# Cross attention: first scores, weighing of the batch ahead and second scores as one block of small products; transposes and low parts moved

## The chip, the cores and the metric

The kernel runs on one core of a Trainium2 chip. The time is device microseconds of one launch; the kernel before took 896.02 us (median of 3 runs, 895.63 to 896.3). The profile is of one further execution of it. Five engines work side by side: TensorE (PE in the profile, its weight loads PEld), VectorE (DVE), ScalarE (ACT), GpSimd (POOL) and SyncE (SP), which only issues transfers here. Each runs its own instructions in order and waits on semaphores for the others.

## The reference

One layer of three blocks with residuals: cross attention of 64 latents a batch to 512 context rows and to themselves, self attention over the 64 latents, and a feed forward part whose inputs and weights are rounded to 4-bit blocks. There are 16 batches, the width is 512. The change touches the first block only:

```python
xn = _ln(x, g_x, b_x)            # the context: 16 x 512 x 512
ln = _ln(latents, g_l, b_l)      # the latents: 16 x 64 x 512
q = ln @ w_q
kv_in = jnp.concatenate([xn, ln], axis=1)
k, v = jnp.split(kv_in @ w_kv, 2, axis=-1)
q, k, v = (split(q) * scale, split(k), split(v))     # 8 heads of 64
sim = jnp.einsum('bhid,bhjd->bhij', q, k)
sim = jnp.where(m, sim, -jnp.finfo(sim.dtype).max)
attn = jax.nn.softmax(sim, axis=-1)
out = jnp.einsum('bhij,bhjd->bhid', attn, v)
return _ln(out @ w_out, g_o, b_o)
```

## The kernel before

The program has three stages. `_latents` makes keys, queries and values of the latents and the context weights; `cross_attention` runs over the 16 batches; `SelfAttention` and `FeedForward` follow, tile by tile of 128 latent rows. The order of the instructions on each engine is the order in which the functions below call them; nothing reorders them between engines except the semaphore waits.

A matrix product to near fp32 is three products of high and low parts (`terms`, L121: high x high, high x low, low x high), with 4 slices of 128 in the inner dimension: twelve matmuls of 128 x 512 make one "full product" below.

In `cross_attention` batch b has:

- `keys(b, m)`, m = 0 to 3: a full product of two heads' keys, 128 x 512 (tile `pk`), then VectorE multiplies it with the row of inverse deviations (L911, tile `k`). The first and last 64 columns of `k` are keys of the latents, fetched by `around` (four small transfers for two m). There are six homes for `k`, four of which a batch takes; so the fetch for m = 2, 3 of the next batch must wait for this batch's first scores, and that for m = 0, 1 of the batch after for its second scores.
- `values(b, t)`, t = 0 to 3: a full product of 128 context rows' values (`pv`), which ScalarE scales and copies to `v` (L924).
- `scores(b, a)`, a = 0, 1: 8 small matmuls (16 passes in the trace) of 64 x 64 weights by 288 columns into two score tiles of two banks each (`sim`). a = 0 needs keys 0 and 1, a = 1 keys 2 and 3.
- `softmax(b, a)`: VectorE subtracts, masks and takes the minimum, twice (L956, out of `sim` into `pr`), ScalarE takes the exponential and its sum, twice (L960).
- `turn` and `turn_both`: eight transposes of `pr` in all for each a (`prt`, L171), ScalarE copies them to `prT` (L972). `turn_latents` transposes the latents' part (`prlt`, L989), ScalarE copies it to `prl`.
- `finish(b)`: `weigh`, 40 small matmuls (80 passes) with 128 x 64 tiles into the bank `av` (L1005), then `collect` on VectorE (a reciprocal L1017 and two products L1023).
- every second batch, for a pair `done` of finished batches: `out_turn` (four transposes `ot`, ScalarE's high part `oh` L1038, VectorE's low part `ol` L1041), `out_product` (a full product `po`), `out_norm`, `out_add`.

The eight banks of TensorE's output memory are split in three pools: `ps_mm`, three banks for full products and transposes (`mm`, `tr`); `ps_sim`, two tiles of two banks (`two`); `ps_av`, one bank.

Between these, in the same order, stand the preparation of the next batch's context (`cx.high` on ScalarE, `cx.low` on VectorE for even and on GpSimd for odd slices, L362 and L368; `cx.stats`, L321; `cx.fetch`, `cx.flat`, `cx.every` transfers) and `tick()`, which advances the rounding of the feed forward weights by one step (`Quantise.piece`: VectorE, GpSimd and ScalarE ops L194 to L210 and L287 to L290, two transfers).

The weighing of batch b - 1 happens inside batch b. The order of the small products in a batch before: after keys 0 and 1 the transposes of `pr` 1 and of the latents of batch b - 1 (and `ot`); after keys 2 the weighing of b - 1 and the first scores of b; after keys 3 and values 0 and 1 the transposes of `pr` 0 and the second scores of b.

Of the kernel before, what the change touches and what calls it, by code (L numbers as in the profile page):

```python
# [9 lines left out]
F32 = mybir.dt.float32  # L10
# [9 lines left out]
P = 128  # L20
D = 512
KC = D // P
B = 16
S = 64
N = 512
NJ = N // P
NT = B * S // P
# [18 lines left out]
def f32(t):  # L46

    return t.bitcast(F32)
# [777 lines left out]
def cross_attention(tc, cm, sc, i, cw, cx, w1, w2, att, quant):  # L826

    nc = tc.nc
# [19 lines left out]
    def columns_of(r):  # L848

        first = S * (1 - r)  # L850
        return slice(first, first + N + S), slice(S - first, S - first + N)

    state = {}
# [48 lines left out]
    def keys(b, m):  # L902

        k = ends.pop((b, m))
        hi, lo = cx.done[b]
        cols = slice(m * P, (m + 1) * P)
        ps = cm.mm(f"pk_{b}_{m}")
        cm.product(
            ps, lambda c: (w_k[0][:, c, cols], w_k[1][:, c, cols], hi[:, c, :], lo[:, c, :]), range(KC)
        )  # L910
        nc.vector.tensor_tensor(k[:, S : S + N], ps, cx.row[b], ALU.mult)  # L911
        state[b]["k"].append(k)
# [14 lines left out]
    def scores(b, a):  # L927

        st = state[b]
        st["sim", a] = pss = [cm.two(f"sim_{b}_{a}_{r}") for r in range(2)]  # L930
        for h in range(2):
            for r in range(2):
                rows = slice(r * S, (r + 1) * S)
                at = columns_of(r)[0].start + h * half
                for c in range(2):
                    m = 2 * a + c
                    nc.tensor.matmul(  # L937
                        pss[r][c * S : (c + 1) * S, h, :half],
                        lhsT=queries[b % 2][rows, m, :],
                        rhs=st["k"][m][rows, at : at + half],  # L940
                        start=True,
                        stop=True,
                    )

    def softmax(b, a):
        st = state[b]
        st["pr", a] = w1.tile([P, 2, N + S], F32, tag="pr", bufs=2, name=f"pr_{b}_{a}")

        def two(t):
            return t.rearrange("p (h n) -> p h n", h=2)  # L950

        for r, ps in enumerate(st.pop(("sim", a))):
            mask = masks[b % 2][:, columns_of(r)[0]]
            pr = st["pr", a][:, r, :]
            least = cm.small.tile([P, 1], F32, tag="least", name=f"least_{b}_{a}_{r}")
            nc.vector.tensor_tensor_reduce(  # L956
                two(pr), ps[:, :, :half], two(mask), -1.0, BIG, ALU.add, ALU.min, least
            )
            t = 2 * a + r
            nc.scalar.activation(  # L960
                pr, pr, AF.Exp, bias=least, scale=-1.0, accum_out=st["tot"][:, t : t + 1]
            )

    def turn(b, a, r):
        st = state[b]
        pt = cm.tr(f"prt_{b}_{a}_{r}")
        cm.transpose_chunks(pt, st["pr", a][:, r, columns_of(r)[1]], NJ)
        turned(b, a, r, pt)

    def turned(b, a, r, pt):  # L970
        prT = w1.tile([P, NJ, P], F32, tag="prT", bufs=4, name=f"prT_{b}_{a}_{r}")
        nc.scalar.copy(prT, pt.rearrange("p (j q) -> p j q", q=P))  # L972
        state[b]["prT", a, r] = prT

    def turn_both(b):

        pt = cm.two(f"prt_{b}")
        for r in range(2):
            cm.transpose_chunks(pt[:, r, :], state[b]["pr", 1][:, r, columns_of(r)[1]], NJ)
        for r in range(2):  # L980
            turned(b, 1, r, pt[:, r, :])

    def turn_latents(b):
        st = state[b]
        prl = w2.tile([P, 2, P], F32, tag="two_h", bufs=2, name=f"prl_{b}")
        pt = cm.tr(f"prlt_{b}")[:, : 2 * P].rearrange("p (n q) -> p n q", q=P)
        for a in range(2):
            pr = st.pop(("pr", a)).rearrange("p r t -> p (r t)")
            nc.tensor.transpose(pt[:, a, :], pr[:, N : N + P], cm.ident)  # L989
        nc.scalar.copy(prl, pt)  # L990
        st["prl"] = prl
# [38 lines left out]
    def out_turn(p):  # L1030
        o = state.pop(("o", p))
        pt = cm.tr(f"ot_{p}")
        cm.transpose_chunks(pt, o.rearrange("p a c r d -> p (a c r d)"), KC)
        oh = w1.tile([P, KC, P], F32R, tag="oh", name=f"oh_{p}")
        ol = w2.tile([P, KC, P], F32R, tag="ol", name=f"ol_{p}")
        for k in range(KC):
            src, bias = pt[:, k * P : (k + 1) * P], cw.bv[:, k : k + 1]
            nc.scalar.activation(oh[:, k, :], src, AF.Identity, bias=bias)  # L1038
        for k in range(KC):
            src, bias = pt[:, k * P : (k + 1) * P], cw.bv[:, k : k + 1]  # L1040
            nc.vector.scalar_tensor_tensor(  # L1041
                ol[:, k, :], src, bias, f32(oh[:, k, :]), ALU.add, ALU.subtract
            )
        state["oT", p] = oh, ol

    def out_product(p):
        oh, ol = state.pop(("oT", p))
        po = cm.mm(f"po_{p}")
        cm.product(
            po, lambda k: (oh[:, k, :], ol[:, k, :], w_o[0][:, k, :], w_o[1][:, k, :]), range(KC)  # L1050
        )
        state["po", p] = po, cm.moments(po, f"o_{p}")
# [13 lines left out]
    def out_moments(p):  # L1066
        cm.shift(cm.x[p], f"a_{p}", cm.x_mv[:, p, :])
# [12 lines left out]
    def finish(b):  # L1080
        for a in range(2):
            for r in range(2):
                weigh(b, a, r)
        collect(b)
# [11 lines left out]
    for b in range(B):  # L1096

        def tick():
            if b:
                quant.tick()  # L1100

        done = (b - 3) // 2 if b >= 3 and b % 2 else None
        last = b == B - 1
        keys(b, 0)
        if last:
            att.load("Wq")
            att.load("Wk")
        cx.high(b + 1, 0)
        if b >= 4 and b % 2 == 0:
            out_moments((b - 4) // 2)  # L1110
        if b > 1:
            tick()
        keys(b, 1)
        cx.low(b + 1, 0)
        cx.high(b + 1, 1)
        if b > 1:
            tick()
        if b:
            turn_both(b - 1)
            turn_latents(b - 1)  # L1120
        if done is not None:
            out_turn(done)
        keys(b, 2)
        cx.fetch(b + 2, 0)
        if b == 0:
            for k in range(KC):
                load_o(k)
        cx.flat(b + 1)
        cx.low(b + 1, 1)
        cx.high(b + 1, 2)  # L1130
        tick()
        if last:
            att.split("Wq", 0, 1)
        if b:
            finish(b - 1)
        tick()
        if last:
            att.split("Wq", 2)
        scores(b, 0)
        softmax(b, 0)  # L1140
        around(b + 1, 2, 3)
        keys(b, 3)
        cx.fetch(b + 2, 1)
        cx.low(b + 1, 2)
        cx.high(b + 1, 3)
        tick()
        values(b, 0)
        cx.every(b + 1)
        cx.low(b + 1, 3)
        cx.stats(b + 2, 0)  # L1150
        tick()
        if last:
            att.split("Wq", 3)
            att.load("Wv")
        values(b, 1)
        begin(b + 1)
        latents_values(b + 1)
        cx.fetch(b + 2, 2)
        cx.stats(b + 2, 1)
        tick()  # L1160
        if last:
            att.norm(0)
            att.split("Wk", 0, 1)
        turn(b, 0, 0)
        turn(b, 0, 1)
        scores(b, 1)
        softmax(b, 1)
        around(b + 2, 0, 1)
        if done is not None:
            out_product(done)  # L1170
        tick()
        values(b, 2)
        cx.fetch(b + 2, 3)
        cx.stats(b + 2, 2)
        tick()
        if done is not None:
            out_norm(done)
            out_add(done)
        if b == 0:
            weight_o(0)  # L1180
            weight_o(1)
        if b == 2:
            att.sa.load()
        if b == 5:
            att.sa.work()
        if last:
            att.split("Wk", 2, 3)
            att.load("Wo")
            att.turn(0)
        values(b, 3)  # L1190
        cx.stats(b + 2, 3)
        cx.spread(b + 2)
        mask(b + 1)
        if b == 0:
            weight_o(2)
            weight_o(3)
        quant.tick()
        cx.load(b + 3)
    turn_both(B - 1)
    turn_latents(B - 1)  # L1200
    att.product(0, "Wq")
    att.split("Wv", 0, 1)
# [4 lines left out]
    att.product(0, "Wk")  # L1207
    att.rope(0, "Wk")
    out_turn(NT - 1)
    att.product(0, "Wv")  # L1210
    out_moments(NT - 2)
    att.end(0)
# [678 lines left out]
```

## Time and profile before

| | |
|---|---|
| time, median of 3 runs (range) | 896.02 us (895.63 to 896.3) |
| the profiled execution: time, span from first to last instruction | 895.7 us, 893.9 us |
| two batches of cross attention in its trace (428.67 to 489.80 us) | 61.13 us |
| busy in these: TensorE, weight loads, VectorE, ScalarE, GpSimd | 61.13, 49.17, 50.52, 29.09, 26.20 us |
| granted TensorE clock | 0.999 |
| DMA busy share over these two batches | 0.52 |

A row of the profile's timeline gives start and length in us, engine, line, operation, the tile written and those read, array tile (rows\*columns), output shape and count; a last bracket tells how long the engine had stood idle before and what released it. Cross attention runs from about 84 to 574 us.

### The profile page before, as it was taken

How to read it: one execution, taken by the hardware profiler on the slowest of the kernel's cores; microseconds unless marked ns; L12 is line 12 of the kernel's file. 1: busy time of each engine (PE TensorE's matmuls, PEld its weight loads, DVE VectorE, ACT ScalarE, POOL GpSimd, SP SyncE). 2: the span in 40 equal slices, each digit the busy share in tenths (PEclk: the TensorE clock that was granted, in tenths of full speed). 3: DMA queues.
4: the chain of work that ended last, by engine and by line, in shares of the span. 5: the costliest groups of instructions: out<-in, count | busy, mean ns of one | idle time of the engine just before them, and what ended most of it. 6: DMA issues, size and time to landing. Idle time of an engine off the chain costs nothing.

```text
span 893.9 us, 17187 instructions
## 1 busy us (share of the span) xinstructions
PE 886.8 (99%) x6583; PEld 735.9 (82%) x6583; DVE 693.0 (78%) x1414; ACT 399.8 (45%) x785; POOL 305.7 (34%) x357
## 2 busy tenths in 40 slices
PE   8999999999999999999999999999999999999998
PEld 8998778877887878788778877878888888888887
DVE  7554467798799787786987985588998897888876
ACT  5553544543454445445444544555555323322221
POOL 3244233335253353162453532545444120100000
PEclk9999999999999999999999999999999999999999
DMA  8465554645565456445554442331006530000000
GB/s 294 155 236 165 169 155 138 186 143 154 158 179 144 153 150 176 117 133 156 144 156 152 137 126 97 116 148 43 1 1 251 198 142 13 12 12 12 12 13 24
DMA packets 80378, 111.11 MB, mean 124 GB/s; under 512 B 33176, under 2 KB 39080, under 8 KB 79016
## 3 DMA queue, kind: packets, MB, share of 16 engines
q1 hardware_dynamic: 80136, 109.48, 38.4%
q8 instruction: 52, 0.85, 0.4%
q0 software_dynamic: 160, 0.52, 0.2%
q14 instruction: 30, 0.25, 0.1%
HBM read 84.26 MB, written 25.72 MB: 123 GB/s over the span
## 4 chain that ended last, share of the span: by engine, by line
PE 96%; DVE 2%; POOL 1%; issue 0%; DMA 0%; ACT 0%; POOLq 0%; DVEq 0%; ACTq 0%
PE pk L121 20%; PE pv L121 20%; PE gu L121 14%; PE dn L121 7%; PE av L1005 5%; PE sim L937 4%; PE prt L171 3%; PE po L121 3%; PE Wv L121 2%; PE wo L121 2%; PE lv L121 2%; PE Wq L121 2%; PE Wk L121 2%; PE lq L121 2%; PE lk L121 2%; PE ht L171 1%
## 5 line engine op out<-in xcount | busy, mean ns | idle before, releaser
L121 PE MATMUL pv<-xvh,x 128*128 128x512 f32 x512 | 133.1, 392 | 0.0
L121 PE MATMUL pk<-x,xkh 128*128 128x512 f32 x512 | 130.4, 397 | 0.0
L121 PEld LDWEIGHTS pk<-x,xkh 128*128 128x128 f32 x512 | 93.7, 188 | 25.4 <-issue 3.9
L121 PEld LDWEIGHTS pv<-xvh,x 128*128 128x128 f32 x512 | 95.3, 188 | 23.3 <-issue 1.8
L911 DVE TENSOR_TENSOR k<-pk,row 128x512 f32<-128x512 f32 x64 | 43.9, 685 | 51.9 <-PE pk L121 51.9
L924 ACT ACTIVATE v<-pv,rs 128x512 f32<-128x512 f32 x64 | 43.9, 686 | 78.1 <-PE pv L121 78.0
L960 ACT ACTIVATE pr<-pr,least 128x576 f32<-128x576 f32 x64 | 49.2, 771 | 58.3 <-DVE least L956 56.7
L368 POOL TENSOR_TENSOR x<-raw,x 128x512 fp32r<-128x512 f32 x32 | 43.7, 1365 | 77.4 <-ACT x L362 71.1
L121 PE MATMUL pk<-x,xkl 128*128 128x512 f32 x256 | 68.7, 390 | 0.0
L121 PE MATMUL pv<-xvl,x 128*128 128x512 f32 x256 | 68.5, 389 | 0.0
L121 PE MATMUL gu<-uT,fx 128*128 128x512 f32 (+1 forms) x288 | 66.7, 377 | 0.0
L121 PE MATMUL gu<-gT,fx 128*128 128x512 f32 (+1 forms) x288 | 65.8, 376 | 0.0
L121 PEld LDWEIGHTS gu<-gT,fx 128*128 128x128 f32 x288 | 52.2, 188 | 7.6 <-ACT fx L129 0.2
L121 PEld LDWEIGHTS gu<-uT,fx 128*128 128x128 f32 x288 | 51.9, 188 | 7.2
L121 PEld LDWEIGHTS pk<-x,xkl 128*128 128x128 f32 x256 | 48.0, 188 | 10.4
L121 PEld LDWEIGHTS pv<-xvl,x 128*128 128x128 f32 x256 | 48.1, 188 | 10.2
L956 DVE CUSTOM_DVE_ANT_0 pr<-sim,mask 128x576 f32<-128x576 f32 x64 | 45.9, 754 | 6.5 <-PE sim L937 5.3
L205 ACT ACTIVATE qe_h<-qe_h,mmagic 128x512 f32<-128x512 f32 (+1 forms) x24 | 16.5, 688 | 66.4 <-DVE qe_h L202 64.3
L321 DVE BATCH_NORM_STATS2 cst<-nat 128x6 f32<-128x512 f32 x64 | 42.9, 670 | 3.5 <-DMA nat<-in_ctx_dram 3.5
L121 PE MATMUL dn<-dT,hh 128*128 128x512 f32 x170 | 42.9, 392 | 0.0
L972 ACT COPY prT<-prt 128x512 f32<-128x512 f32 x64 | 34.1, 585 | 18.4 <-PE prt L171 18.4
L1005 PEld LDWEIGHTS av<-v,prT 128*64 128x64 f32 x1024 | 36.7, 138 | 5.6 <-issue 5.6
(339 smaller groups left out, 1959.0 us busy)
## 6 DMA issues: line engine op xcount, KB each, us to landing
nat<-in_ctx_dram SPq DMA_DIRECT2D x16, 1024.0 KB
raw<-in_ctxT_dram SPq DMA_DIRECT2D x64, 256.0 KB
d_d<-qhl_d SPq DMA_DIRECT2D x11, 512.0 KB
row<-rs_d SPq DMA_DIRECT2D x16, 256.0 KB
g_d<-qhl_g SPq DMA_DIRECT2D x8, 512.0 KB
u_d<-qhl_u SPq DMA_DIRECT2D x8, 512.0 KB
gT<-g_d SPq DMA_DIRECT2D x4, 1024.0 KB
uT<-u_d SPq DMA_DIRECT2D x4, 1024.0 KB
```

The lines of the kernel that those rows point to most:

```text
L121: self.nc.tensor.matmul(ps, lhsT=p[i], rhs=p[j], start=start and n == 0, stop=stop and n == last)
L171: self.nc.tensor.transpose(pt[:, c * P : (c + 1) * P], src[:, c * P : (c + 1) * P], self.ident)
L205: nc.scalar.activation(e, e, AF.Relu, bias=self.mmagic, scale=MAGIC)
L321: nc.vector.bn_stats(st, self.nat[b][:, j, :])
L368: by.tensor_tensor(lo, self.raw[:, c, :], f32(hi), ALU.subtract)
L911: nc.vector.tensor_tensor(k[:, S : S + N], ps, cx.row[b], ALU.mult)
L924: nc.scalar.mul(v, ps, cx.rs[b][:, t : t + 1])
L937: nc.tensor.matmul(pss[r][c * S : (c + 1) * S, h, :half], lhsT=queries[b % 2][rows, m, :], rhs=st["k"][m][rows, at : at + half], start=Tru ...
L956: nc.vector.tensor_tensor_reduce(two(pr), ps[:, :, :half], two(mask), -1.0, BIG, ALU.add, ALU.min, least)
L960: nc.scalar.activation(pr, pr, AF.Exp, bias=least, scale=-1.0, accum_out=st["tot"][:, t : t + 1])
L972: nc.scalar.copy(prT, pt.rearrange("p (j q) -> p j q", q=P))
L1005: nc.tensor.matmul(st["av"][rows, 2 * a + r, :], lhsT=w[:, rows], rhs=v[:, at : at + S], start=(n == 0), stop=(n == len(pairs) - 1),)
```

## The change

The two forms of turning `pr` become one, `turn(b, a)`, whose eight transposes go into one score tile. `turn_latents` uses the bank of the weighing. `out_turn` is split: its VectorE part becomes `out_low`. In the loop over the batches:

- `turn(b - 1, 1)`, `turn_latents(b - 1)` and `out_turn` move from behind keys 1 to behind keys 0; `out_low` stands behind keys 1.
- first scores, weighing of b - 1 and second scores stand together behind keys 3 and ahead of values 0, with both `around` fetches behind them. (Batch 0, with nothing to weigh, has its first scores behind keys 2, its second behind values 0.)
- `turn(b, 0)` stays behind values 1, without the second scores; one `tick()` moves from behind `finish` to behind `turn(b, 0)`; in the last batch `att.split("Wq", 2)` moves behind keys 3.

```diff
@@ -961,29 +961,21 @@
                 pr, pr, AF.Exp, bias=least, scale=-1.0, accum_out=st["tot"][:, t : t + 1]
             )
 
-    def turn(b, a, r):
-        st = state[b]
-        pt = cm.tr(f"prt_{b}_{a}_{r}")
-        cm.transpose_chunks(pt, st["pr", a][:, r, columns_of(r)[1]], NJ)
-        turned(b, a, r, pt)
-
-    def turned(b, a, r, pt):
-        prT = w1.tile([P, NJ, P], F32, tag="prT", bufs=4, name=f"prT_{b}_{a}_{r}")
-        nc.scalar.copy(prT, pt.rearrange("p (j q) -> p j q", q=P))
-        state[b]["prT", a, r] = prT
-
-    def turn_both(b):
-
-        pt = cm.two(f"prt_{b}")
+    def turn(b, a):
+
+        pt = cm.two(f"prt_{b}_{a}")
         for r in range(2):
-            cm.transpose_chunks(pt[:, r, :], state[b]["pr", 1][:, r, columns_of(r)[1]], NJ)
+            cm.transpose_chunks(pt[:, r, :], state[b]["pr", a][:, r, columns_of(r)[1]], NJ)
         for r in range(2):
-            turned(b, 1, r, pt[:, r, :])
+            prT = w1.tile([P, NJ, P], F32, tag="prT", bufs=4, name=f"prT_{b}_{a}_{r}")
+            nc.scalar.copy(prT, pt[:, r, :].rearrange("p (j q) -> p j q", q=P))
+            state[b]["prT", a, r] = prT
 
     def turn_latents(b):
         st = state[b]
         prl = w2.tile([P, 2, P], F32, tag="two_h", bufs=2, name=f"prl_{b}")
-        pt = cm.tr(f"prlt_{b}")[:, : 2 * P].rearrange("p (n q) -> p n q", q=P)
+        pt = cm.ps_av.tile([P, D], F32, tag="av", name=f"prlt_{b}")[:, : 2 * P]
+        pt = pt.rearrange("p (n q) -> p n q", q=P)
         for a in range(2):
             pr = st.pop(("pr", a)).rearrange("p r t -> p (r t)")
             nc.tensor.transpose(pt[:, a, :], pr[:, N : N + P], cm.ident)
@@ -1036,15 +1028,18 @@
         for k in range(KC):
             src, bias = pt[:, k * P : (k + 1) * P], cw.bv[:, k : k + 1]
             nc.scalar.activation(oh[:, k, :], src, AF.Identity, bias=bias)
+        state["oT", p] = oh, ol, pt
+
+    def out_low(p):
+        oh, ol, pt = state["oT", p]
         for k in range(KC):
             src, bias = pt[:, k * P : (k + 1) * P], cw.bv[:, k : k + 1]
             nc.vector.scalar_tensor_tensor(
                 ol[:, k, :], src, bias, f32(oh[:, k, :]), ALU.add, ALU.subtract
             )
-        state["oT", p] = oh, ol
 
     def out_product(p):
-        oh, ol = state.pop(("oT", p))
+        oh, ol, _ = state.pop(("oT", p))
         po = cm.mm(f"po_{p}")
         cm.product(
             po, lambda k: (oh[:, k, :], ol[:, k, :], w_o[0][:, k, :], w_o[1][:, k, :]), range(KC)
@@ -1110,16 +1105,18 @@
             out_moments((b - 4) // 2)
         if b > 1:
             tick()
+        if b:
+            turn(b - 1, 1)
+            turn_latents(b - 1)
+        if done is not None:
+            out_turn(done)
         keys(b, 1)
+        if done is not None:
+            out_low(done)
         cx.low(b + 1, 0)
         cx.high(b + 1, 1)
         if b > 1:
             tick()
-        if b:
-            turn_both(b - 1)
-            turn_latents(b - 1)
-        if done is not None:
-            out_turn(done)
         keys(b, 2)
         cx.fetch(b + 2, 0)
         if b == 0:
@@ -1131,18 +1128,23 @@
         tick()
         if last:
             att.split("Wq", 0, 1)
-        if b:
-            finish(b - 1)
-        tick()
-        if last:
-            att.split("Wq", 2)
-        scores(b, 0)
-        softmax(b, 0)
-        around(b + 1, 2, 3)
+        if b == 0:
+            scores(b, 0)
+            softmax(b, 0)
         keys(b, 3)
         cx.fetch(b + 2, 1)
         cx.low(b + 1, 2)
         cx.high(b + 1, 3)
+        if last:
+            att.split("Wq", 2)
+        if b:
+            scores(b, 0)
+            softmax(b, 0)
+            finish(b - 1)
+            scores(b, 1)
+            softmax(b, 1)
+            around(b + 1, 2, 3)
+            around(b + 2, 0, 1)
         tick()
         values(b, 0)
         cx.every(b + 1)
@@ -1152,6 +1154,11 @@
         if last:
             att.split("Wq", 3)
             att.load("Wv")
+        if b == 0:
+            scores(b, 1)
+            softmax(b, 1)
+            around(b + 1, 2, 3)
+            around(b + 2, 0, 1)
         values(b, 1)
         begin(b + 1)
         latents_values(b + 1)
@@ -1161,11 +1168,8 @@
         if last:
             att.norm(0)
             att.split("Wk", 0, 1)
-        turn(b, 0, 0)
-        turn(b, 0, 1)
-        scores(b, 1)
-        softmax(b, 1)
-        around(b + 2, 0, 1)
+        turn(b, 0)
+        tick()
         if done is not None:
             out_product(done)
         tick()
@@ -1196,7 +1200,7 @@
             weight_o(3)
         quant.tick()
         cx.load(b + 3)
-    turn_both(B - 1)
+    turn(B - 1, 1)
     turn_latents(B - 1)
     att.product(0, "Wq")
     att.split("Wv", 0, 1)
@@ -1207,6 +1211,7 @@
     att.product(0, "Wk")
     att.rope(0, "Wk")
     out_turn(NT - 1)
+    out_low(NT - 1)
     att.product(0, "Wv")
     out_moments(NT - 2)
     att.end(0)
```

## The prediction

> **What bounds the kernel now.** I read the page from the top: busy shares, clock row, chain of waits; then TensorE's timeline over one batch, then VectorE's over the next, because the change reorders one engine and leans on the other.
>
> ```profile
> PE 886.8 (99%) x6583; PEld 735.9 (82%) x6583; DVE 693.0 (78%) x1414; ACT 399.8 (45%) x785; POOL 305.7 (34%) x357
> PEclk9999999999999999999999999999999999999999
> PE 96%; DVE 2%; POOL 1%; issue 0%; DMA 0%; ACT 0%; POOLq 0%; DVEq 0%; ACTq 0%
> ```
>
> TensorE is busy 99% of the span at the full granted clock and is 96% of the chain. So time is won only by making its stream shorter, and lost only by making it wait. The stream, batch b = 10 (start, length, what):
>
> ```profile
> 388.81 1.03 PE L171 MATMUL prt<-ident,pr 128*128 128x128 f32 x8
> 389.69 0.38 PE L989 MATMUL prlt<-ident,pr 128*128 128x128 f32 x2
> 389.82 2.09 PE L121 MATMUL pk<-x,xkh 128*128 128x512 f32 x8
> ...
> 392.75 0.57 PE L1005 MATMUL av<-v,prT 128*64 128x64 f32 x12
> ...
> 395.23 1.20 PE L937 MATMUL sim<-k,mask 64*64 64x288 f32 x16
> 396.36 2.11 PE L121 MATMUL pk<-x,xkh 128*128 128x512 f32 x8
> ...
> 399.23 1.07 PE L121 MATMUL pv<-xvh,x 128*128 128x512 f32 x4
> ...
> 404.68 1.03 PE L171 MATMUL prt<-ident,pr 128*128 128x128 f32 x8
> 405.64 1.20 PE L937 MATMUL sim<-k,mask 64*64 64x288 f32 x16
> 406.77 1.20 PE L121 MATMUL pv<-xvh,x 128*128 128x512 f32 x4
> ...
> 412.35 1.98 PE L121 MATMUL pk<-x,xkh 128*128 128x512 f32 x8
> ```
>
> Read starts, not lengths (matmuls overlap). The 24 key products from 412.35 end where the next transposes start, 417.79: 5.44 us, 0.2267 each, 2.72 for a product of twelve. Whatever a stretch takes beyond that is the price of small products and of going in and out of them. The full-array products need no help; what the array's tile (128\*128, 128\*64, 64\*64 in the rows) changes to is what costs.
>
> **The change, part by part.** First TensorE, before:
>
> - 388.81 to 392.75: 3.94, less 2.72 = 1.22 for ten transposes and the way into the 128\*64 tile. Of that the way in is about 0.08: the first 36 key products of batch 0 (83.88 to 92.13) take 8.25 against 36 x 0.2267 = 8.16, so 0.09 into 64\*64; and transposes cost 0.11 each (388.81 to 389.69) plus 0.06 at their edge (four of them and a product, 576.76 to 579.98: 3.22 - 2.72 = 0.50).
> - weighing 2.48, scores 1.13, way back to full tiles 399.23 - 396.36 - 2.72 = 0.15.
> - eight transposes with the way into scores 0.96, scores 1.13, way back 412.35 - 406.77 - 5.44 = 0.14.
>
> Sum 1.22 + 2.48 + 1.13 + 0.15 + 0.96 + 1.13 + 0.14 = 7.21; check: 417.79 - 388.81 - 96 x 0.2267 = 7.22.
>
> After: ten transposes before a full product 1.22 - 0.08 = 1.14; one block, way in 0.09 + scores 1.13 + weighing 2.48 + scores 1.13 + way back 0.14 = 4.97; eight transposes followed by a full product 8 x 0.11 + 0.06 = 0.94. Sum 7.05, so **0.16 us a batch**, 15 batches with a block: 2.4 us. Batch 0 has no weighing, and its second scores lose their neighbour: + 0.09 + 0.14 + 0.94 - 0.96 - 0.14 = + 0.07.
>
> The scores-to-weighing change of tile isn't in the trace. The stream holds 1.13 from the scores' start to the next start after them whichever full product follows, and weighing takes 2.48 whether scores (395.23) or a full product (573.90) follows, so the leaving price sits inside the group; I take 0 extra. Ends: - 0.09 (the 0.09 of a way in is saved) and + 0.15 (as a way back to full tiles), that is - 1.4 to + 2.3 us over 15 batches. The Trainium skill, "TensorEngine Tiling", Key Properties, says that a change of tiling mode, not of tile, drains the engine. By that rule alone I would count changes: five a batch before, four after, and with the 0.09 to 0.15 of the rows one fewer is worth 1.4 to 2.3 us. The segments give a little more, as the transposes no longer touch a change; I take the rows.
>
> Three weighings (batches 3, 5, 7) last 2.69 instead of 2.48: the 4 latent products wait for ScalarE's `prl` copy, which ended at 177.53 in batch 3, the product starting at 177.59. It was late because ScalarE stood 2.94 us before L205. Now the copies follow keys(b, 0), with three key products and scores between (9.4 us) and L205 ordered behind them: **3 x 0.21 = 0.6 us** gone, and nothing else is late there.
>
> Sum: - 2.4 + 0.1 - 0.6 = - 2.9 us. The profiled execution took 895.7 (span 893.9, 1.8 around it), so 892.8; the median 896.02 lies 0.3 above it, so **893.1** for a median.
>
> Now what the order makes wait. The score buffers are two, of two banks. Before, each pair of scores had a full product or more until the next user of these buffers. Now the second scores need both back from VectorE's L956 during the weighing, 2.48 us. Here the Trainium skill speaks against the change: "TensorEngine Tiling", PSUM Bottleneck: tiling quickens TensorE, not the emptying of PSUM. L956 is 0.75 each, 0.68 from start to start, so 1.4 of 2.48 if VectorE is there in time; by the rule the emptying would set the pace. VectorE before, in batch 11:
>
> ```profile
> 423.40 1.12 DVE L1041 SCALAR_TENSOR_TENSOR ol<-ot,bv,oh 128x128 fp32r<-128x128 f32 x4 [3.13 <-ACT oh L1038]
> 424.44 0.68 DVE L911 TENSOR_TENSOR k<-pk,row 128x512 f32<-128x512 f32 x1
> ...
> 426.73 0.85 DVE L1023 TENSOR_TENSOR o<-av,rt 64x256 f32<-64x256 f32 x2
> ...
> 429.16 0.76 DVE L956 CUSTOM_DVE_ANT_0 pr<-sim,mask 128x576 f32<-128x576 f32 x1
> ```
>
> Scores ended at 425.80, L956 starts at 429.16 and the second ends at 430.6: 4.8 us late, free of charge then. It is late because of 3.13 us before L1041 (22.1 us over its eight occurrences), then L1023 and a quantise reduction (1.5). The edit takes all three from in front: out_turn comes a product earlier, with `oh` ahead of L205 on ScalarE (copies 1.06 + 0.38, `oh` 1.16: 2.6 after `ot`, while L1041 is due 3.4 after it, behind keys(b, 1)); collect follows L956; one quantise step moves behind the block. Odd batch by rows, from the end of keys(b, 1): L911 0.6, L1041 1.0, low 0.6, quantise 1.0: 3.3; L911 3.9; row transpose and two quantise ops 1.4: 5.3; keys(b, 3) ends at 5.44: L911 6.1, low 6.7; scores end 5.44 + 0.09 + 1.13 = 6.66: L956 done 7.4 and 8.1; weighing ends 9.15. **About 1 us to spare.** Even batches have a reduction (1.3) in place of L1041 and the same end. Single VectorE ops are sometimes 1.1 us longer (L207 0.69 median, 1.78 at most): one is absorbed, two are not; I allow + 0.2 us in all.
>
> The other moves, all hidden. `ot` holds a product bank until L1041, about 4.5 us after it; keys(b, 3) wants it at 5.4. `prlt` sits in the weighing's bank, read 9 us before weighing. `prt_0` in a score buffer needs the second scores' L956, due 1.5 after them and wanted 5.6 after. VectorE then stands idle about 1 us before collect and 0.4 before the last L956; ScalarE has four exponentials ahead of the first value copy, 0.4 us late with two products of cover. SP: eight key-end DMAs of 0.57 us stand together, the first four free at the first scores' end, the last at the second's; behind them row, mask, queries and `vl`, 2.3 to 6 us after the block, are wanted 14 us after it or later; a quantise load lands about 1 us before its reduction, and if late costs VectorE time behind the block. GpSimd's clearing of `vl` waits for the later weighing, with quantise multiplies queued behind, 34% busy. In the last batch att.split("Wq", 2), 0.69 on VectorE, goes ahead of L956, where no `low` stands.
>
> **Rivals.**
>
> - *VectorE late* (slower): what speaks for it is the 4.8 above, against it the order worked out. It decides from 2.48 us after the first scores on. If the odd batches keep 4.8: 7 x 2.3 = 16, time 893 + 16 = 909; two slow ops in each odd batch, 2.2 against 1 to spare, give 7 x 1.2 = 8 and 901.
> - *Small waits eat it* (no change): 0.2 us in each of 15 batches, the size of the three waits seen, or 0.15 at the new tile change: 893.1 + 2.3 to 3.0 = 895.4 to 896.1.
> - *It doesn't shorten the stream*: TensorE's order follows the text of the change, all 15 blocks adjacent, so only the prices could be wrong; inside the bounds above.
>
> **How the numbers follow.** Forecast as worked out 0.64, its own range 891.5 to 894.2; small waits 0.15, 894.2 to 897.8; VectorE late 0.21, of it a third under 899.5. I say 893.1 + 0.2 = 893.3, range 891.4 to 899.5. Two thousandths, 1.8 us, is about what this kernel's measurement can tell from no change: under 894.2 is faster.
>
> **What would show it.** Right: in TensorE's timeline scores, weighing, scores start at 0, 1.13, 3.61 from each other, the next value product at 4.74, batch pairs 0.32 shorter (61.14 before, 60.8 after), no weighing over 2.48. Wrong: a gap between weighing and second scores with VectorE L956 named (rival one); weighing starting later than 1.13 after the first scores (tile change dearer); L956 starting over 1 us after the first scores' end; waits of keys(b, 3) on L1037, which is L1041 now.

## The result and the profile after

The kernel after takes **900.69 us** (median of 5 runs, 899.17 to 901.35) against 896.02 (895.63 to 896.3): ratio 1.0049, 95% interval 1.0038 to 1.006. It is slower, by 0.5%; 893.3 was forecast, with a range up to 899.5. One execution, of the kernel with three edits below, took 1780.45 us, with products of TensorE 0.44 us from start to start instead of 0.23; its profile is not used, and the ratio given there is that of the others. The profiled execution took 901.35 us with a span of 899.4. From its page, the busy shares, the clock row and the first row of the chain of waits:

```profile
PE 888.6 (99%) x6583; PEld 738.4 (82%) x6583; DVE 687.3 (76%) x1414; ACT 399.9 (44%) x785; POOL 307.0 (34%) x357
...
PEclk9999999999999999999999999999999999999999
...
PE 85%; DVE 6%; DMA 3%; ACT 3%; POOL 1%; issue 1%; SPq 1%; ACTq 0%; DVEq 0%; POOLq 0%
```

The busy shares look as before. The chain is what differs: it was 96% TensorE, and now 15% of it runs over other engines, as it goes back from each wait of TensorE along the engine that ended it. The waits of TensorE after, by what released it (total us, times, longest):

```profile
PE sim L937 <- DVE least L956: 3.4, 3, 1.4
...
PE prt L171 <- DVE least L956: 0.7, 1, 0.7
```

This view shows where to look but not the sum, since part of a wait hides in longer groups. TensorE's timeline after, batch 5:

```profile
242.48 1.20 PE L937 MATMUL sim<-k,mask 64*64 64x288 f32 x16
243.61 0.57 PE L997 MATMUL av<-v,prT 128*64 128x64 f32 x12
...
245.88 0.29 PE L997 MATMUL av<-v,prT 128*64 128x64 f32 x4
247.58 1.86 PE L937 MATMUL sim<-k,mask 64*64 64x288 f32 x16 [1.42 <-DVE least L956]
249.38 1.93 PE L121 MATMUL pv<-xvh,x 128*128 128x512 f32 x4
251.11 1.91 PE L121 MATMUL pv<-xvl,x 128*128 128x512 f32 x4
```

From start to start: scores to weighing 1.13, as forecast; weighing to second scores 3.97 instead of 2.48; second scores to the value product 1.80 instead of 1.13; and then value products of four matmuls that take 1.73 from start to start instead of 0.9 to 1.0. The first two differences are one cause seen twice: the second scores fill two score tiles, their first passes wait until the first L956 has read its tile, and passes for the other tile wait for the second L956, 0.68 us later. The same three differences, batch by batch (batch 0 has no block; there its eight transposes wait for L956):

| batch | waits in the block, us (before the second scores + within them) | beside it |
|---|---|---|
| 0 | | 0.84 before the transposes |
| 3 | 0.99 + 0.66 | |
| 5 | 1.49 + 0.66 | 1.6 of slower matmuls |
| 7 | 0.10 + 0.66 | |
| 13 | 1.14 + 0.66 | |
| 9, 10, 15 | 0.17, 0.15, 0.54 (within) | |
| 1, 2, 4, 6, 8, 11, 12, 14 | 0 | |

The sum is 9.7 us. The profiled execution less this sum is 891.7 us, even a little less than was forecast for a kernel without waits (892.8); the last kernel below whose blocks wait for nothing took 891.49. So the stream did get shorter, and the time went into VectorE reaching L956 too late. Why it is late in batch 5 is in the timelines of the other engines after. VectorE:

```profile
235.77 0.71 DVE L287 STREAM_TRANSPOSE qhl_g<-qw_g 128x512 f32<-128x512 f32 x1 [0.76 <-POOL qw_g L210]
237.15 0.69 DVE L911 TENSOR_TENSOR k<-pk,row 128x512 f32<-128x512 f32 x1 [0.67 <-PE pk L121]
239.50 1.13 DVE L1037 SCALAR_TENSOR_TENSOR ol<-ot,bv,oh 128x128 fp32r<-128x128 f32 x4 [1.66 <-ACT oh L1030]
240.54 1.35 DVE L368 TENSOR_TENSOR x<-raw,x 128x512 fp32r<-128x512 f32 x1
...
245.62 1.23 DVE L368 TENSOR_TENSOR x<-raw,x 128x512 fp32r<-128x512 f32 x1
246.77 0.74 DVE L956 CUSTOM_DVE_ANT_0 pr<-sim,mask 128x576 f32<-128x576 f32 x1
```

ScalarE:

```profile
232.46 0.62 ACT L362 CAST x<-raw 128x512 fp32r<-128x512 f32 x1
236.56 0.62 ACT L288 CAST qhl_g<-qhl_g 128x512 fp32r<-128x512 f32 x1 [3.48 <-DVE qhl_g L287]
237.09 1.07 ACT L971 COPY prT<-prt 128x512 f32<-128x512 f32 x2
238.04 0.38 ACT L982 COPY prl<-prlt 128x256 f32<-128x256 f32 x1
238.30 1.17 ACT L1030 ACTIVATE oh<-ot,bv 128x128 fp32r<-128x128 f32 x4
```

GpSimd:

```profile
240.05 1.29 POOL L368 TENSOR_TENSOR x<-raw,x 128x512 fp32r<-128x512 f32 x1 [3.29 <-ACT x L362]
245.24 1.06 POOL L210 TENSOR_TENSOR qw_g<-qw_g,qs_g 128x512 f32<-128x512 f32 x1 [3.90 <-DVE qw_g L208]
```

Read the three together. A quantise step issued ahead of the early transposes puts the rounding copy L288 into ScalarE's queue ahead of `prT`, `prl` and `oh`. It waits for VectorE's L287, which waits for GpSimd's L210. So `oh` ends at 239.47, VectorE stands 1.66 us before `ol`, and everything behind `ol` on VectorE is late. Then its two low products (L368) take 1.35 and 1.23 us instead of 0.68, each beside a GpSimd operation that was running when it started (to 241.34 and 246.30) and each ending 0.55 us after it. L956 starts at 246.77, 3.1 us after the scores' end at 243.68.

Collected over the batches and all kernels below, the second scores cost no extra time as long as the second L956 ends no later than 2.36 us after the first scores' end: 2.35 cost nothing, 2.40 cost 0.04, 2.53 cost 0.17, 2.90 cost 0.54. In batch 5 it ended 4.5 after.

### The profile page after: what moved, and what is told of

It reads as the page before. It is cut to its first block, busy times and chain, and to the rows that moved or that the text cites. A ratio compares the mean times of both kernels' runs of the same rounds, so it can differ in the third digit from the quotient of the medians.

```text
span 899.4 us, 17167 instructions
## 1 busy us (share of the span) xinstructions
PE 888.6 (99%) x6583; PEld 738.4 (82%) x6583; DVE 687.3 (76%) x1414; ACT 399.9 (44%) x785; POOL 307.0 (34%) x357
## 4 chain that ended last, share of the span: by engine, by line
PE 85%; DVE 6%; DMA 3%; ACT 3%; POOL 1%; issue 1%; SPq 1%; ACTq 0%; DVEq 0%; POOLq 0%
PE pv L121 16%; PE pk L121 15%; PE gu L121 13%; PE dn L121 6%; PE sim L937 4%; PE av L997 4%; PE prt L171 3%; PE Wv L121 2%; PE wo L121 2%; PE lv L121 2%; PE po L121 2%; PE Wq L121 2%; PE Wk L121 2%; PE lq L121 2%; PE lk L121 2%; PE ht L171 1%
## 5 line engine op out<-in xcount | busy, mean ns | idle before, releaser
L121 PE MATMUL pv<-xvh,x 128*128 128x512 f32 x512 | 135.9, 397 | 0.0
L121 PE MATMUL pk<-x,xkh 128*128 128x512 f32 x512 | 128.3, 393 | 0.0
L368 POOL TENSOR_TENSOR x<-raw,x 128x512 fp32r<-128x512 f32 x32 | 46.7, 1461 | 43.0 <-ACT x L362 43.0
L956 DVE CUSTOM_DVE_ANT_0 pr<-sim,mask 128x576 f32<-128x576 f32 x64 | 45.8, 751 | 2.9 <-PE sim L937 2.1
L205 ACT ACTIVATE qe_h<-qe_h,mmagic 128x512 f32<-128x512 f32 (+1 forms) x24 | 16.5, 687 | 66.4 <-DVE qe_h L202 64.2
L321 DVE BATCH_NORM_STATS2 cst<-nat 128x6 f32<-128x512 f32 x64 | 42.8, 669 | 3.5 <-DMA nat<-in_ctx_dram 3.5
L937 PE MATMUL sim<-k,mask 64*64 64x288 f32 x512 | 41.9, 416 | 3.4 <-DVE least L956 3.4
```

The lines of the kernel that those rows point to most:

```text
L121: self.nc.tensor.matmul(ps, lhsT=p[i], rhs=p[j], start=start and n == 0, stop=stop and n == last)
L205: nc.scalar.activation(e, e, AF.Relu, bias=self.mmagic, scale=MAGIC)
L321: nc.vector.bn_stats(st, self.nat[b][:, j, :])
L368: by.tensor_tensor(lo, self.raw[:, c, :], f32(hi), ALU.subtract)
L937: nc.tensor.matmul(pss[r][c * S : (c + 1) * S, h, :half], lhsT=queries[b % 2][rows, m, :], rhs=st["k"][m][rows, at : at + half], start=Tru ...
L956: nc.vector.tensor_tensor_reduce(two(pr), ps[:, :, :half], two(mask), -1.0, BIG, ALU.add, ALU.min, least)
```

## The experiments

Two candidates for the lateness stand side by side in these rows, the queue of ScalarE and the slow low products, and a third reading is possible: that the block with two score buffers is simply too tight. Each edit below is to the kernel after unless it says otherwise.

**The quantise step behind the early transposes.**

```diff
-        if b > 1:
-            tick()
         if b:
             turn(b - 1, 1)
             turn_latents(b - 1)
         if done is not None:
             out_turn(done)
+        if b > 1:
+            tick()
         keys(b, 1)
```

> One edit to the kernel after: the first quantise step of a batch is issued behind turn, turn_latents and out_turn instead of ahead of them, so that ScalarE meets its quantise copy (L288, which stood 3.48 us for VectorE's L287 in batch 5) behind prT, prl and oh. Theory A (VectorE's scores are late because that quantise copy heads ScalarE's queue, and oh, and with it ol and all of VectorE behind it, come late): the idle time of VectorE before ol (1.2 to 1.7 us in batches 3, 5 and 13) goes, L956 in these batches starts 1.2 to 1.7 us nearer to its scores, and the waits before second scores there (1.14 to 1.49 now) fall to 0.3 or nothing, with the later 0.66 gone or halved: 3 to 5 us, so 895.5 to 897.5. Rival B (VectorE is late because its low products run 1.2 to 1.7 us instead of 0.68 beside GpSimd's): the idle time may go, but the waits before second scores stay within 0.3 of what they are, 899.5 to 901.3. Rival C (the place of the quantise step only moves the lateness: L287's own wait for GpSimd falls between ol and low instead): waits of 1 us or more stay in the same batches, 900 to 902.

**893.37 us** (893.18 to 893.5; ratio to the kernel before 0.9967, 0.9955 to 0.998). Better than the 895.5 to 897.5 of theory A. ScalarE in batch 5 of this kernel:

```profile
232.91 0.39 ACT L982 COPY prl<-prlt 128x256 f32<-128x256 f32 x1
233.17 1.17 ACT L1030 ACTIVATE oh<-ot,bv 128x128 fp32r<-128x128 f32 x4
234.18 0.67 ACT L288 CAST qhl_g<-qhl_g 128x512 fp32r<-128x512 f32 x1
```

and VectorE:

```profile
235.98 1.12 DVE L1037 SCALAR_TENSOR_TENSOR ol<-ot,bv,oh 128x128 fp32r<-128x128 f32 x4
237.02 0.68 DVE L368 TENSOR_TENSOR x<-raw,x 128x512 fp32r<-128x512 f32 x1
...
241.43 1.23 DVE L368 TENSOR_TENSOR x<-raw,x 128x512 fp32r<-128x512 f32 x1
242.59 0.74 DVE L956 CUSTOM_DVE_ANT_0 pr<-sim,mask 128x576 f32<-128x576 f32 x1
```

`oh` ends before `ol` is due (no bracket of idle time), and with ScalarE free earlier GpSimd's low is over (at 236.74) when VectorE's first starts: it takes 0.68 again. Both gains together bring L956 to 0.68 us after the scores' end in batch 5 (241.91). The waits of batches 3, 5 and 7 are gone, and 0.04 is left in batch 13; what is left is 0.54 in batch 15, 0.17 and 0.21 in 9 and 10, and batch 0. That the edit also ended the first slow low there, and with the wait the 1.6 us of slower matmuls in batch 5, is why the 3 to 5 us expected were too few.

**The even low product behind the block.** `cx.low(b + 1, 2)`, the second L368 above, moves behind the second `softmax` (batch 0 as it was).

```diff
-        cx.low(b + 1, 2)
+        if b == 0:
+            cx.low(b + 1, 2)
...
             scores(b, 1)
             softmax(b, 1)
+            cx.low(b + 1, 2)
             around(b + 1, 2, 3)
```

> One edit to the kernel after: in batches with a block cx.low(b+1, 2) is issued behind the second softmax instead of ahead of the block, so that L956 of the first scores no longer stands behind a low that takes 0.68 or 1.23 to 1.67 us. Theory A (oh late is the main cause, low a smaller one): L956 starts 0.7 earlier in most batches and 1.2 earlier in batches 3, 5, 7 and 13, which need 1.5, 2.0, 0.7 and 1.7 to lose their waits: the waits before second scores fall from 5.5 us in all to about 1.5, 896 to 898. Rival B (slowed low products are the main cause): waits before second scores vanish, 893.5 to 895.5. If what is moved comes late for its own reader instead (key or value products of the next batch waiting for the low part), the time stays above 899 with new waits in the products of the next batch.

**896.34 us** (895.27 to 898.04; ratio 1.0002, 0.9994 to 1.001): theory A's range. VectorE in batch 5 of this kernel:

```profile
238.84 1.13 DVE L1037 SCALAR_TENSOR_TENSOR ol<-ot,bv,oh 128x128 fp32r<-128x128 f32 x4 [2.01 <-ACT oh L1030]
239.88 1.35 DVE L368 TENSOR_TENSOR x<-raw,x 128x512 fp32r<-128x512 f32 x1
...
244.96 0.75 DVE L956 CUSTOM_DVE_ANT_0 pr<-sim,mask 128x576 f32<-128x576 f32 x1
```

The idle time before `ol` is still there, and L956 is 2.3 us late. Batches 3, 5, 7 and 13 still wait, 0.57 to 1.36 us each. Taking away work in front of L956 helps as much as that work is long; the queue of ScalarE stays.

**Both, and batch 0.** In batch 0 the second scores' L956 stood behind a statistics operation that waited for a transfer. From VectorE's timeline after:

```profile
101.92 0.69 DVE L321 BATCH_NORM_STATS2 cst<-nat 128x6 f32<-128x512 f32 x1 [3.54 <-DMA nat<-in_ctx_dram]
...
102.79 0.76 DVE L956 CUSTOM_DVE_ANT_0 pr<-sim,mask 128x576 f32<-128x576 f32 x1
```

The third edit issues it behind the second `softmax` of batch 0:

```diff
-        cx.stats(b + 2, 0)
+        if b:
+            cx.stats(b + 2, 0)
...
         if b == 0:
             scores(b, 1)
             softmax(b, 1)
+            cx.stats(b + 2, 0)
```

> The two edits together, and in batch 0 cx.stats(2, 0) issued behind the second softmax (there L956 stood behind L321, which waited 3.54 us for a transfer; 0.84 us of TensorE). Theory A and B together (all of the loss is VectorE reaching L956 too late, and the adjacent block itself is as short as its segments): no wait over 0.1 us before any second scores, batch pairs of 60.7 to 60.8 us throughout, time 891.5 to 893.5, below the kernel before. Rival C (two score buffers are too few for two adjacent scores whatever stands ahead of VectorE): waits of 0.3 us or more remain in several batches, 895 or more.

> The kernel with all three edits once more, for a profile at the usual clock: span 890.2 to 890.9, time 892.1 to 892.9; every L956 within 0.2 of its scores' end but in batch 15 perhaps, no wait of TensorE for L956 over 0.1, pairs of batches of 60.7 to 60.8.

**892.39 us** (median; ratio 0.9957, 0.9943 to 0.997) and, run again, **892.11** (891.98 to 892.27; 0.9955, 0.9941 to 0.9968). Rival C falls: two score buffers are enough. TensorE in that profile, the starts of batches 11 and 13:

```profile
409.54 1.98 PE L121 MATMUL pk<-x,xkh 128*128 128x512 f32 x8
...
470.21 1.98 PE L121 MATMUL pk<-x,xkh 128*128 128x512 f32 x8
```

From start to start 60.67 us for two batches, and every pair from the third batch on takes exactly that. From batch 1 on each L956 starts within 0.1 us of its scores' end and nothing waits for it; batch 15 is the exception, with 1.47 and the 0.54 of wait that it had before.

The third edit alone:

> One edit to the kernel after: in batch 0 cx.stats(2, 0), whose first instruction waited 3.54 us for a transfer ahead of L956, is issued behind the second softmax. If the 0.84 us that TensorE lost in batch 0 came from that, it goes and nothing else moves: 0.8 us less, 899.5 to 900.2. If the transposes of batch 0 wait for something else as well, no gain: 900.4 to 901.2.

**899.65 us** (899.06 to 901.08; ratio 1.0041, 1.0029 to 1.0054), 1.0 less than after, and the wait in batch 0 is gone from its trace; waits of batches 3, 5, 7 and 13 differ from those after by up to 0.6 each way, so the 0.84 is read from the trace rather than from the time.

**The second scores back where they were.** The second scores, their softmax and the `around` for the batch after return behind the transposes that follow value product 1; these transposes go into two product banks again (that part of the edit, and batch 0, which goes back too, are not shown). First scores and weighing stay together.

```diff
             finish(b - 1)
-            scores(b, 1)
-            softmax(b, 1)
             around(b + 1, 2, 3)
-            around(b + 2, 0, 1)
...
         turn(b, 0)
+        scores(b, 1)
+        softmax(b, 1)
+        around(b + 2, 0, 1)
```

> The kernel after with the second scores, their softmax and around(b+2, 0, 1) put back behind the transposes that follow the second value product; first scores, weighing and all else stay. If the loss is only the wait of the second scores for the score buffers: no wait for L956 is left although VectorE is as late as in the kernel after (L956 still 1 to 3 us behind the first scores' end in batches 3, 5, 13), the short stream is given up too (5 changes of tile instead of 4), so the time is near that of the kernel before, 895 to 896.5. If adjacent scores and weighing, or the early transposes, cost something themselves, it stays above 898.

**895.51 us** (895.34 to 896.35; ratio 0.9992, 0.9984 to 1.0). VectorE is still late, though less so (L956 1.55 us after the scores' end in batches 3, 5, 7 and 13; the second L956 ends 2.97 to 2.99 after it, 0.6 past the 2.36), and nobody waits for it. All pairs from the third batch on take 61.21 us, against 61.14 for a pair without waits before. So the early transposes, the moved low part and first scores next to weighing cost next to nothing by themselves; what costs is a second user of the score buffers 2.48 us after the first.

**Is it ScalarE's queue, or the place of the step?** Moving the step moves its VectorE and GpSimd operations too. Here the step stays, and only its copy changes engine:

```diff
-        nc.scalar.copy(hi, f32(lo))
+        nc.vector.tensor_copy(hi, f32(lo))
```

> One edit to the kernel after: the rounding copy of a quantise piece (L288) is done by VectorE, right behind its L287, instead of by ScalarE. The step stays where it was. Theory A (what makes oh late is that this copy stands in ScalarE's queue ahead of prT, prl and oh and waits for VectorE): ScalarE does oh as soon as ot is there, ol has no idle time before it, L956 comes 1 us or more nearer to its scores in batches 3, 5 and 13, and the time falls to 892.8 to 895, near the 893.4 of the kernel with the step moved. Rival D (the step's place matters by what it puts into VectorE's and GpSimd's queues ahead of ol and L956, not by ScalarE's): VectorE has 0.6 us more to do there, L956 stays as late or later, 900 to 902.5.

**895.21 us** (894.69 to 896.45; ratio 0.9991, 0.9983 to 0.9999). It misses theory A's range by 0.2 and lies 4.8 below the near end of rival D's. In every odd batch the idle time before `ol` is 0, though the step stands where it did, so it is ScalarE's queue. What is left comes from the other side: VectorE now has that copy to do, in the even batches too, and L956 is 2.0 and 1.6 us late in batches 4 and 6. Among what stands ahead of it in batch 4 of this kernel, in VectorE's timeline:

```profile
212.56 1.37 DVE L288 CAST qhl_u<-qhl_u 128x512 fp32r<-128x512 f32 x1
```

VectorE's median for this copy is 0.43 to 0.47 (ScalarE's 0.62); here it takes 1.37, beside GpSimd's low (212.37 to 213.64). Batches 4, 5 and 6 then wait 1.10, 1.02 and 0.62 us, and 12 and 14 0.2 each.

**The same edit to the kernel before.** There the step in front of the transposes is another, whose L205 stood 2.94 us at the head of ScalarE's queue.

```diff
-        if b > 1:
-            tick()
         if b:
             turn_both(b - 1)
             turn_latents(b - 1)
         if done is not None:
             out_turn(done)
+        if b > 1:
+            tick()
         keys(b, 2)
```

> The kernel before with the same kind of edit: the quantise step that is issued ahead of its transposes (its L205 stood 2.94 us at the head of ScalarE's queue) goes behind out_turn. Theory A: before, that lateness cost only the waits of the weighing for prl, 0.21 in batches 3, 5, 7 and 13; these go: 895.2 to 895.9, so nearly all of the gain of the moved step in the kernel after (7.3 us) belongs to the adjacent block, which cannot bear the lateness. Rival E (the moved step is a gain of its own, by shorter queues everywhere): 892 to 894 here too, and then the adjacent block itself brings nothing.

**894.94 us** (894.77 to 895.73; ratio 0.9987, 0.998 to 0.9993), 0.3 better than the range. Rival E falls: the moved step gives 1.3 us to the kernel before and 7.3 to the kernel after. In this trace L956 of the odd batches from 3 on is still 1.9 to 3.2 us behind its scores, free of charge; the four longer weighings (2.69) are 2.48, and all pairs take 61.14. Against the kernel with three edits (892.11) this is the fair measure of the block: 2.8 us (the other two edits end waits that this kernel does not have).

**The last wait.** In batch 15 a weight split of 0.69 us stands ahead of L956; it goes behind the second `softmax`, on top of the three edits.

```diff
-        if last:
-            att.split("Wq", 2)
         if b:
             scores(b, 0)
...
             cx.low(b + 1, 2)
+            if last:
+                att.split("Wq", 2)
```

> The kernel with all three edits, and in batch 15 att.split('Wq', 2), 0.69 us of VectorE ahead of the first scores' L956 (1.47 late there, 0.54 us of wait before the value product), issued behind the second softmax. If what remains of the waits obeys the same rule (second scores start on time while the second L956 ends within 2.36 us of the first scores' end), this last wait goes: 0.5 us less than the 892.1 to 892.4 of the kernel with three edits, so 891.5 to 892.0, and every block of the kernel takes 1.13, 2.48 and 1.13. If the split then comes late for its own reader, the Wq products, no gain: 892.1 or more.

**891.49 us** (891.46 to 892.39; ratio 0.9947, 0.9934 to 0.9961). All blocks now take 1.13, 2.48 and 1.13. This is the fastest kernel of the study.

**Why are the low products slow?** Two tries to take GpSimd's low from beside VectorE's.

```diff
-        cx.low(b + 1, 1)
+        if b == 0:
+            cx.low(b + 1, 1)
...
-        cx.fetch(b + 2, 1)
+        if b == 0:
+            cx.fetch(b + 2, 1)
...
             softmax(b, 1)
+            cx.low(b + 1, 1)
+            cx.fetch(b + 2, 1)
             around(b + 1, 2, 3)
```

> One edit to the kernel after: GpSimd's low product cx.low(b+1, 1), which in batches 3, 5, 7 and 13 stands beside VectorE's low (L368, 1.35 there instead of 0.68), is issued behind the second softmax, with the transfer that refills its source behind it. The quantise step stays where it was, so oh comes as late as before. If VectorE's op is slow because GpSimd's runs beside it: the first low takes 0.7 in these batches, L956 comes 0.6 to 0.7 earlier, the idle time before ol (1.2 to 1.7) stays, so the waits before second scores fall by 0.6 to 0.7 a batch in batches 3, 5, 7 and 13: 2.5 us, with or without the 1.6 of the lower clock, so 896.5 to 898.7. If the op is slow for another reason (its source, its place): still 1.2 to 1.35, and 899.5 to 901.5.

**899.47 us** (898.77 to 900.41; ratio 1.0037, 1.0023 to 1.0051), and no answer: between the old place and the new one there is no other GpSimd instruction, so the low starts at 240.11 in batch 5 as ever. Moving a call in the text moves nothing on an engine that has nothing to be moved past. The second try adds, for all batches but the first, VectorE in place of GpSimd for this product:

```diff
-            by = (self.cm.nc.vector, self.cm.nc.gpsimd)[c % 2]
+            by = (self.cm.nc.vector, self.cm.nc.gpsimd)[c == 3 or (c == 1 and b == 1)]
```

> The kernel with GpSimd's low moved in the text left GpSimd's order as it was (its low still ran at 240.11 in batch 5, beside VectorE's). Here this low product, cx.low(b+1, 1), is done by VectorE behind the second softmax, so that nothing of GpSimd stands beside VectorE's first low in batches 3, 5, 7 and 13; the quantise step stays. If VectorE's op is slow because GpSimd's runs beside it: the first low takes 0.7 there, the idle time before ol (1.0 to 1.7) stays, L956 comes 0.6 to 0.7 earlier, and the waits before second scores fall by 0.6 to 0.7 in each of these batches, 2.5 us less: 896.5 to 898.7. If it is slow for another reason: still 1.35, 899 to 901.5.

VectorE's two low products ahead of L956 in batch 5 of this kernel:

```profile
254.07 0.68 DVE L368 TENSOR_TENSOR x<-raw,x 128x512 fp32r<-128x512 f32 x1
...
258.48 1.23 DVE L368 TENSOR_TENSOR x<-raw,x 128x512 fp32r<-128x512 f32 x1
```

The first low takes 0.68 in every odd batch from 3 on, though `ol` still comes late (2.45 us of idle time in batch 5), so it is GpSimd's low beside it that slowed it; the second, which the edit leaves as it was, still takes 1.23 in most of them, beside GpSimd's L210. The time, **940.43 us** (938.0 to 943.02; ratio 1.0486, 1.0472 to 1.0501), says nothing on this, as the edit did something else as well: the transfer behind the low waits for VectorE at the head of SyncE's queue. SyncE's waits in this kernel, then in the kernel after:

```profile
SPq L354 <- DVE x L368: 149.3, 28, 7.4
```

```profile
SPq L354 <- DVE x L368: 87.3, 14, 8.1
```

28 such waits instead of 14. VectorE then stands for the loads of the quantise pieces (27.2 us before L194 of the gate weights alone, up to 6.0 at a time), and the block with it. That these loads are late because they queue behind the moved transfer is what the rows suggest; no run tried the two apart.

## Why the prediction was wrong

**The stream: right, and too small.** Scores, weighing and scores start at 0, 1.13 and 3.61 and the value product at 4.74 in every undisturbed batch; scores to weighing costs no extra, which the trace of before could not show. The term 0.16 us a batch was under-sized: without waits a pair takes 60.67 against 61.14, that is 0.235 a batch and 3.5 in 15 batches instead of 2.4 (the other way of counting, by changes of tile, gave 1.4 to 2.3, further off). About 0.05 of the difference is the eight transposes ahead of a full product, 0.89 instead of 0.94.

**The weighing waits: right.** They are gone after; they were four (batch 13 too), 0.8 instead of 0.6. The kernel before loses them with one moved step, and 0.4 more.

**"`oh` ahead of L205 on ScalarE (copies 1.06 + 0.38, `oh` 1.16: 2.6 after `ot`, while L1041 is due 3.4 after it": this step failed.** It freed `oh` from one quantise copy and did not ask which stands in front of the new place. It was there to be seen; ScalarE's timeline before, batch 5:

```profile
232.85 0.62 ACT L288 CAST qhl_g<-qhl_g 128x512 fp32r<-128x512 f32 x1 [2.30 <-DVE qhl_g L287]
...
236.93 0.73 ACT L205 ACTIVATE qe_g<-qe_g,mmagic 128x512 f32<-128x512 f32 x1 [2.94 <-DVE qe_g L202]
```

Both stood and waited; the change took the transposes' copies from behind the second and put them behind the first. `oh` came 5.4 us after `ot` instead of 2.6. Part of this could not be read off: L287 started 3.5 us after keys(b, 0) began in batch 5 before and 5.85 after. There VectorE had stood 1.92 us for a transfer and 0.73 for ScalarE, in another quantise piece, ahead of the statistics whose part on GpSimd comes before L210 in its queue.

**"About 1 us to spare": the size that fell with it.** The sum said that L956 is done 7.4 and 8.1 us after the end of keys(b, 1), with weighing's end at 9.15. In batch 5 of the kernel after it was 10.6 and 11.2, 3.2 later: `ol` started 2.55 after keys(b, 1) instead of 0.6 (1.95), and the two low products, "low 0.6" each in the sum, took 0.7 and 0.55 more from start to start. The limit was also nearer: 2.36 us after the scores' end rather than 2.48. With the queue mended the odd batches 3, 5 and 7 had 0.26 to spare (2.10), and with the low moved 0.87 (1.49), close to the 1 us forecast.

**"I allow + 0.2 us in all" for slow VectorE operations: wrong.** They were not chance. The low products are slow where a GpSimd operation runs at the same time, and that is fixed by the order: the same two in batches 3, 5, 7 and 13, every time, as long as the queue is as it is. The first could be read off too; the sum takes "low 0.6" where VectorE's timeline before has 1.10 in batches 3, 5, 7 and 13, beside GpSimd's low (in batch 5 to 235.36):

```profile
234.79 1.10 DVE L368 TENSOR_TENSOR x<-raw,x 128x512 fp32r<-128x512 f32 x1
```

The Trainium skill, "SBUF — State Buffer", Who interferes with whom, describes the shared port pair of VectorE and GpSimd as an exclusive lock; the rows agree (0.68 alone; 1.10, 1.23 and 1.35 beside GpSimd, each time ending 0.53 to 0.55 after GpSimd's operation, as if it had waited for it). Two such meetings ahead of L956 are 1.2 us, which is more than the spare that was claimed.

**Batch 0 at + 0.07: wrong by 0.84.** `prt_0` "wanted 5.6 after" holds for a block; batch 0 has one value product there, and L321's wait for its transfer stood in front.

**The rival that came** is VectorE late with "two slow ops in each odd batch", priced at 901. The place is right, and both its signs came: the gap with L956 named, and L956 over 1 us late. That its price comes so near the 900.69 is in good part luck: it counted 1.2 us in each of seven odd batches, 8 in all; four of them lost 6.4 in the profiled execution, three others 0.9, batch 0 lost 0.8 and the slower matmuls 1.6, and the largest part of the lateness was a wait for ScalarE, not a slow operation. The 3.13 us before L1041, its evidence, was taken as removed because one of ScalarE's two waits was.

## What to carry to other kernels

When work moves forward on one engine, list for every other engine that it uses which instruction stands directly ahead of the new place, and what that one waits for; a wait that cost nothing there is paid by what now stands behind it. When two users of a buffer move together, the time between them becomes a deadline: sum the producer's queue up to the releasing instruction at the durations of busy stretches, and put everything that can wait behind it. Then the short stream pays: the same block is 4.7 us slower than the kernel before, or 4.9 faster (891.49 against 896.37 in the same set) with four calls moved behind what was waiting on them.

## What the hardware showed

After the wait in batch 5 of the kernel after, matmuls ran at about half speed. Windows of TensorE's timeline after (stretch, its length, busy times, the granted clock and the DMA share):

```profile
245.90:249.40 3.50, 2.08 (x27) 0.83 (x22) 3.35 (x9) 1.63 (x4) 2.08 (x2) 1.00 0.71 229
249.38:253.30 3.92, 3.92 (x12) 3.12 (x11) 3.78 (x11) 1.63 (x4) 1.08 (x2) 0.56 0.12 27
253.30:257.30 4.00, 4.00 (x22) 3.34 (x22) 2.01 (x5) 1.74 (x3) 0.45 (x1) 1.00 0.62 168
```

The granted clock is 0.56 in the middle stretch; the dip itself lasts 3.4 us at 0.5 and costs 1.6 us, more than the 1.42 us of idle time ahead of it. In the same profile waits of about 1 us in batches 3 and 13 were not followed by one, so a wait of this size can be charged twice, but need not be. The kernel with only batch 0 mended has one such stretch as well, behind its longest wait (1.60 us before the second scores of batch 3; the value product there takes 4.45 instead of 2.85). The kernels whose waits before second scores stayed at 1.34 or less have none inside the attention. In the kernel of 940.43 us a wait of 2.57 in batch 7 had none behind it. What decides it, no run shows. The page's clock row, a 9 in every slice, does not show it; the windows do.
